# A sparse graph-attention kernel: image tiles, table order, pacing and width of the row gathers in one change

## Chip, cores, metric

The kernel runs on one core of a Trainium2 chip, as one program. The metric is the device time of one execution in microseconds (us).

## What is computed

The input is a feature matrix x (3327 x 128, fp32) and a matrix adj (3327 x 3327) of which about 2% of the entries are not zero. Layer 0 is a four-head attention over the graph, layer 1 a graph convolution; each works on normalised features and adds to x.

```
h = relu(layernorm(x))
for each head:                               # w1, w2, a, Wlin differ by head
    E   = leaky_relu((h @ w1)[:, None] + (h @ w2)[None, :])   # for each pair of nodes
    s   = exp(8 * tanh((E @ a) / 8)) * adj
    out = leaky_relu((s / s.sum(-1)) @ h @ Wlin.T)
x = x + concat(out of the heads) @ w
h = relu(layernorm(x))
A = D^-1/2 (adj + I) D^-1/2
x = x + relu(A @ (h @ W.T + b))
```

## The kernel before

**Tiling.** Nodes are padded to NP = 3328, which makes NB = 26 blocks of 128 destination rows. Only the non-zero entries of adj are worked on. Each block is done in two halves of 64 rows (`hb` 0 and 1). A half has four fetches of eight tiles (`w` 0 to 3, the tile `g`: 128 partitions x 8 x 720 floats) and one fetch of three tiles for overfull rows (`ge`). In a tile of `g`, partition p holds one neighbour of one of 8 destination rows: 8 rows with 16 neighbours each. Tile t of a half therefore belongs to its rows 8t to 8t+7.

**Tables.** What a neighbour contributes lies as one row of 720 floats (2880 bytes) in DRAM, in `tables[0]` for half 0 and `tables[1]` for half 1. Columns 0 to 63 are the adjacency weights towards the 64 destination rows of the present half, 64 to 191 the features, 192 to 195 a term of the score, 196 a one (for the sum), 197 to 207 more ones that nothing uses, 208 (`PROJ`) to 719 the projection by w2 for four heads. The columns from 64 on are written once, in the opening; columns 0 to 63 are written again for each block by `weights(b, hb)` (L554), one DRAM to DRAM transfer of 3328 rows of 256 bytes on the SP queue, which waits until the gathers of the block before have read that table.

**Gathers.** `gather` (L538) puts into a Python queue one `indirect_dma_start` per tile, eight for a `g` and three for a `ge`, in all 26 x 70 = 1820; on POOL they are one instruction each (L548), and in the steady state POOL does nothing else. There are four `g` buffers and one `ge`. `fetch` (L770) starts the next fetch when a buffer is counted free (`allow`, after the last matmul on it, L645 or L663).

**Pacing.** A hand-written loop walks through 26 x 2 x 9 groups and calls `slot()` six times in each, 108 times in a block; this fixes the program order on all engines. In each slot `trickle` (L795) hands out gathers from the queue at `RATE = 0.7` per slot, and `issue` (L788) makes each of them wait on the newest VectorE instruction of the main line:

```
made = make()
if what is not None and state["pace"] is not None:
    tc.add_manual_dep(made.ins, state["pace"], SYNC, reason="pace")
```

`state["pace"]` is the last L585, so a gather is not issued ahead of the VectorE work that stands before it in program order.

**Main line.** `stage_z` (L562) transposes the gathered projections on TensorE (L573) and VectorE takes the maximum with the destination's projection (L585); `stage_r` (L591) reduces it to scores on TensorE (L597); `finish` (L601) does tanh, exp, weights and the aggregation (L605 to L663); `close` ends a block. Between these steps `advance` runs `prep(b, k)` for the next block in 72 steps: transposes of adj (L349), the lists of neighbours (`cand`, `lists`, L399 to L451) and the indices `idx` (L442) and `idxo` (L511) for the gathers.

**Opening.** Before the first gather, the images of the table rows are made in seven groups of four blocks (the last has two): `norm` (L914; the centred features `cen` of the later blocks on POOL, L930), `features(i)` (L949: `img`, L953 and L955), `turn(i)`, `products(i)` (L971: projections, copies to `img`, L987) and `store(i, t)` (L967: image i to table t, L969). The tile `img` has five buffers. `products(i)` stores image i to table 0 and image i-1 to table 1; `weights(0, 0)` and `weights(0, 1)` come before all of them on the SP queue, and the load of the adjacency of block 1, `load(1)` (L336), after all of them. These tiles lie in the pool `pre`, and the four `g` buffers (pool `pg`) take the room that `pre` gives back. In its first fetches the kernel empties the queue without pacing.

**Tail.** After the last block, layer 1 reads strips of the transposed adjacency into the same `g` buffers and multiplies (L870).

Of the kernel before, what the change touches and what calls it, by code (L numbers as in the profile page):

```python
# [15 lines left out]
P = 128  # L16
# [46 lines left out]
OVT = 3  # L63
ROW = 720
FEAT = 64
PROJ = 208
WORK = 133
# [160 lines left out]
def _sparse_layers(tc, nc, x, adj, w1, w2, a, wlin, w, gw, gb, gb_sb, gwT, x_sb, dinv, flag, ident, out):  # L228
# [24 lines left out]
    with ExitStack() as l0:  # L253
# [18 lines left out]
        hoff = res.tile([P, 2], F32, name="hoff")  # L272
        lower = res.tile([P, P], F32, name="lower")
        rowid = res.tile([P, 1], F32, name="rowid")

# [14 lines left out]
        nc.gpsimd.iota(code, [[-1, NP]], base=NP, channel_multiplier=0, allow_small_or_imprecise_dtypes=True)  # L290
        nc.gpsimd.iota(epos, [[-P, 2 * OVT]], base=2 * NP, channel_multiplier=-1, allow_small_or_imprecise_dtypes=True)


# [44 lines left out]
        def prep(b, k):  # L338
# [6 lines left out]
            def tables_step(j0):  # L345
                n = min(4, NB - j0)
                pt = ps_tr.tile([P, 4, P], F32, name="tr")
                for q in range(n):
                    nc.tensor.transpose(pt[:, q, :], adjb[:, (j0 + q) * P:(j0 + q + 1) * P], ident)  # L349
                at = pat.tile([P, 4, P], F32, name="at") if b else blks[0].pool.tile([P, 4, P], F32, name="at0", bufs=4)  # L350
                nc.scalar.copy(at[:, :n, :], pt[:, :n, :])  # L351
                at0 = (b // 4) * NP
                eng = nc.scalar if b else nc.sync
                eng.dma_start(AT_d[at0 + j0 * P:at0 + (j0 + n) * P, b % 4 * P:b % 4 * P + P].rearrange("(b p) c -> p b c", p=P),
                                  at[:, :n, :])
                js = range(min(n, finished(b) - j0))
                if len(js):
                    known.append(known_step(j0, js, at))
# [56 lines left out]
            k.turned = True  # L415
            hTb = pb.tile([P, P], F32, name="hTb")
            nc.sync.dma_start(hTb, hT_d[:, b * P:(b + 1) * P])
            nc.scalar.activation(adjb, adjb, AF.Copy, accum_out=deg)
# [22 lines left out]
            idx = pb.tile([P, NW, 16], mybir.dt.int32, name="idx")  # L441
            nc.vector.tensor_scalar(idx, pm[:, :64].rearrange("p (c t) -> p c t", c=4), -1.0, float(NP), op0=OP.mult, op1=OP.add)  # L442
            k.idx = idx
# [66 lines left out]
            idxo = pb.tile([P, 2, OVT], mybir.dt.int32, name="idxo")  # L510
            nc.vector.tensor_scalar(idxo.rearrange("p c t -> p (c t)"), hits, -1.0, float(NP), op0=OP.mult, op1=OP.add)  # L511
            k.idxo, k.ex = idxo, ex
# [21 lines left out]
            nc.scalar.copy(pex, pm[:, :16 * H].rearrange("p (t h) -> p t h", h=H))  # L534
            k.x1b, k.x1n, k.pex, k.hTb = x1b, x1n, pex, hTb
            yield

        def gather(b, hb, w):  # L538

            k = blks[b]  # L540
            tab = tables[hb]
            if w == NW:
                g, n, at = pe_.tile([P, OVT, ROW], F32, name="ge"), OVT, k.idxo[:, hb]
            else:
                g, n, at = pg.tile([P, WT, ROW], F32, name="g"), WT, k.idx[:, w, WT * hb:WT * hb + WT]

            def one(t):
                return nc.gpsimd.indirect_dma_start(out=g[:, t, :], out_offset=None, in_=tab[:, :],  # L548
                                                    in_offset=bass.IndirectOffsetOnAxis(ap=at[:, t:t + 1], axis=0))

            queue.extend((k, hb, w, partial(one, t)) for t in range(n))
            k.g[hb, w] = g
# [9 lines left out]
        def stage_z(k, hb, m, slot):  # L562
# [4 lines left out]
            for hp in range(2):  # L567
# [13 lines left out]
                if m == 8:  # L581
                    nc.scalar.activation(r[:, :, :n], z[:, :, :n], AF.Relu)  # L582
                else:
                    r0 = HALF * hb + 32 * (m % 2)
                    made = nc.vector.tensor_tensor(r.rearrange("p h (i s) -> p h i s", s=16), z.rearrange("p h (i s) -> p h i s", s=16),  # L585
                                            k.x1n[:, 2 * hp:2 * hp + 2, r0:r0 + 32, None].to_broadcast([P, 2, 32, 16]), OP.max)
                    state["pace"] = made.ins.name
                out.append(r)
# [165 lines left out]
        state = {"slot": 0, "fetched": 0, "g": 4, "ge": 1}  # L754
        state["pace"], state["credit"] = None, 0.0
        RATE = 0.7
        SYNC = mybir.DependencyInfo(mybir.DependencyClass.Sync, mybir.DependencyReason.DATA)
        ends, tails = [], []
# [29 lines left out]
        def issue():  # L788

            what, _, _, make = queue.popleft()  # L790
            made = make()
            if what is not None and state["pace"] is not None:
                tc.add_manual_dep(made.ins, state["pace"], SYNC, reason="pace")

        def trickle():  # L795
            state["credit"] = min(2.0, state["credit"] + RATE) if queue else 0.0
            while queue and (state["credit"] >= 1 or queue[0][0] is None):
                state["credit"] -= queue[0][0] is not None
                issue()
# [20 lines left out]
        def strip(s, j0, n):  # L820
            g = pg.tile([P, WT, ROW], F32, name="g")
            v = g.rearrange("p t c -> p (t c)")[:, :n * 4 * P].rearrange("p (j i) -> p j i", j=n)
# [60 lines left out]

        with tc.tile_pool(name="pre", bufs=1) as pre:
            blks[0].pool = pre
            w2_sb = pre.tile([P, H, D], F32, name="w2_sb")
            nc.scalar.dma_start(w2_sb, w2.rearrange("h k d -> k h d"))
            a_bc = pre.tile([P, H, D], F32, name="a_bc")
            spans = [(lo, min(hi, NB)) for lo, hi in ((0, 4), (4, 12), (12, NB)) if lo < NB]
            x_v = x.rearrange("(b p) d -> p b d", p=P)  # L890
            for lo, hi in spans:
# [16 lines left out]
            wa = pre.tile([P, 3 * H], F32, name="wa")  # L908
            zero = pre.tile([1, ROW // 6], F32, name="zero")
            nc.vector.memset(zero, 0.0)  # L910
            nc.sync.dma_start(tables[0][NP:NP + 1, :].rearrange("r (k u) -> r k u", k=6), zero[:, None, :].to_broadcast([1, 6, ROW // 6]))
            nc.sync.dma_start(tables[1][NP:NP + 1, :].rearrange("r (k u) -> r k u", k=6), zero[:, None, :].to_broadcast([1, 6, ROW // 6]))

            def norm(b0, n):  # L914
# [10 lines left out]
                for _ in inv_root(rstd, var):  # L925
                    pass
                cen = pre.tile([P, n, D], F32, name=f"cen{b0}")
                for k in range(n):
# [6 lines left out]
            def weights_of_scores():  # L935


                prod = pre.tile([P, H, D], F32, name="prod")
                nc.vector.tensor_mul(prod, w2_sb, a_bc)
# [9 lines left out]
            def features(i):  # L949

                b0, n = 4 * i, min(4, NB - 4 * i)
                img = pre.tile([P, 4, ROW - FEAT], F32, name="img", bufs=5)
                nc.gpsimd.memset(img[:, :n, P + H:PROJ - FEAT], 1.0)  # L953
                cen, rstd = normed.pop(b0)
                nc.vector.tensor_mul(img[:, :n, :P], cen, rstd[:, :, None].to_broadcast([P, n, D]))  # L955
                imgs[i] = img

            def turn(i):
                b0, n = 4 * i, min(4, NB - 4 * i)
                pt = ps_s.tile([P, BANK], F32, name="s")  # L960
                for k in range(n):
                    nc.tensor.transpose(pt[:, k * P:(k + 1) * P], imgs[i][:, k, :P], ident)
                hTs[i] = pre.tile([P, BANK], F32, name="hT", bufs=2)
                nc.scalar.copy(hTs[i][:, :n * P], pt[:, :n * P])
# [6 lines left out]
            def products(i):  # L971
# [13 lines left out]
                for k0, pz in zip(range(0, n, 2), pzs):  # L985
                    m = min(2, n - k0)
                    nc.scalar.copy(img[:, k0:k0 + m, PROJ - FEAT:], pz[:, :m, :])  # L987
                nc.scalar.copy(img[:, :n, P:P + H], px[:, :n, :H])
                nc.scalar.copy(p_all[:, b0:b0 + n, :], px[:, :n, H:])
                store(i, 0)  # L990
                if i:
                    store(i - 1, 1)

            wlin_sb = pre.tile([P, H, D], F32, name="wlin_sb")
            nc.sync.dma_start(wlin_sb, wlin.rearrange("h o d -> o h d"))
# [23 lines left out]
            with tc.manual_schedule():  # L1019
# [17 lines left out]
                weights(0, 0)  # L1037
                weights(0, 1)
                turn(0)
                weights_of_scores()  # L1040
                if len(spans):
# [8 lines left out]
                for i in range(1, K):  # L1050
# [3 lines left out]
                    advance(2 + NCODE * i / (K - 1))  # L1054
                    ahead(i + 4)
                store(K - 1, 1)
                advance(NLIST)
                turn_parameters()
                if NB > 1:
                    load(1)  # L1060
                advance(NPREP)

        pg = l0.enter_context(tc.tile_pool(name="pg", bufs=4))

# [165 lines left out]
```

## Time and profile before

| | |
|---|---|
| time, median of 3 runs | 2569.97 us (2569.47 to 2570.88) |
| time of the profiled execution | 3185.3 us, span 3183.6 us |
| busy: PE / DVE / ACT / POOL | 2551.2 / 2055.1 / 691.6 / 1801.2 us |
| granted TensorE clock, mean | 0.912 |
| moved by DMA | 867.74 MB, of it 671.04 MB by the gathers (q0) |
| gathers | 1664 of `g`, 980 ns mean, and 156 of `ge`, 948 ns mean |
| first and last gather | 86.7 us and 3043.4 us |

The profiled execution took 615 us more than the median, so the stages of the profile are longer than those of a plain run by a quarter on average, and waits in it need not be waits of a plain run. "Busy" of POOL is the time in which it makes the descriptors of a gather; when the data have landed is seen from the DMA packets.

### The profile page before, as it was taken

What the parts mean: (1) busy time and instruction counts of PE and PEld (TensorE: products, weight loads), DVE (VectorE), ACT (ScalarE), POOL (GpSimd) and SP (SyncE); (2) the same over time, 40 slices, a digit from 0 to 9 for tenths busy, and PEclk for the clock granted to TensorE, in tenths of its full rate; (3) what the DMA queues carried; (4) which work ended last, traced back from release to release, by engine and by line L of the source; (5) the groups of instructions that cost most, each with busy time, mean ns of one, the idle gap of its engine ahead of it and who ended that gap; (6) DMA issues with size and microseconds to landing.
All of it is one profiled execution on the core that took longest, in us unless ns stands there. A gap on an engine that the chain in (4) does not pass through costs nothing.

```text
span 3183.6 us, 52428 instructions
## 1 busy us (share of the span) xinstructions
PE 2551.2 (80%) x19410; PEld 1758.0 (55%) x19410; DVE 2055.1 (65%) x6256; ACT 691.6 (22%) x1648; POOL 1801.2 (57%) x1865
## 2 busy tenths in 40 slices
PE   5478778878877878887888888788888888888788
PEld 3355555555555655555555565566655556555544
DVE  6466666667676766766667676776666766765432
ACT  3122222122222222222222221222222222221110
POOL 2456565665666666665656566556555655656610
PEclk8688999989999999998999988999899999999899
DMA  9888898888889888888988888888898887988776
GB/s 325 273 272 264 273 290 254 280 286 281 256 284 295 259 285 283 274 269 280 300 248 284 287 258 278 286 272 262 274 282 251 278 286 247 289 255 242 247 257 235
DMA packets 459768, 867.74 MB, mean 273 GB/s; under 512 B 208877, under 2 KB 317937, under 8 KB 456177
## 3 DMA queue, kind: packets, MB, share of 16 engines
q0 software_dynamic: 145600, 671.04, 64.4%
q1 hardware_dynamic: 217360, 136.76, 15.3%
q10 hardware_dynamic: 96544, 56.50, 5.8%
q8 instruction: 156, 2.56, 0.3%
q14 instruction: 108, 0.88, 0.1%
HBM read 795.84 MB, written 112.63 MB: 285 GB/s over the span
## 4 chain that ended last, share of the span: by engine, by line
PE 52%; DVE 16%; another core or an unknown queue 15%; issue 8%; ACT 5%; DMA 2%; POOL 1%; DVEq 0%; ACTq 0%; POOLq 0%; SPq 0%
PE z L573 20%; PE s L597 9%; DVE r L585 8%; PE tr L614 4%; PE z L576 3%; PE z L870 3%; PE ag L645 2%; ACT r L582 2%; DVE cand L399 2%; PE tr L364 1%; PE tr L349 1%; PE ag L663 1%; PE tr L496 1%; ACT ssb L605 1%
## 5 line engine op out<-in xcount | busy, mean ns | idle before, releaser
L548 POOL DMA_INDIRECT g<-table,idx x1664 | 1630.7, 980 | 1113.5 <-issue 429.4
L573 PE MATMUL z<-ident,g 128*128 128x128 f32 x6656 | 1033.0, 301 | 285.6 <-issue 153.0
L585 DVE TENSOR_TENSOR r<-z,x1n 128x1024 f32<-128x1024 f32 x832 | 1013.0, 1219 | 253.4 <-remote 120.8
L573 PEld LDWEIGHTS z<-ident,g 128*128 128x128 f32 x6656 | 845.4, 156 | 499.8 <-issue 249.4
L597 PE MATMUL s<-r,sel 128*32 128x512 f32 (+1 forms) x3744 | 542.0, 617 | 9.3 <-issue 7.0
L617 DVE TENSOR_TENSOR sc<-tr,g 128x32 f32<-128x32 f32 x208 | 39.5, 190 | 645.3 <-PE tr L614 448.9
L614 PE MATMUL tr<-ident,ssb 128*128 128x128 f32 x988 | 181.8, 311 | 164.3 <-ACT ssb L605 110.0
L605 ACT COPY ssb<-s 128x512 f32<-128x512 f32 x260 | 147.0, 565 | 666.0 <-PE s L597 349.5
L614 PEld LDWEIGHTS tr<-ident,ssb 128*128 128x128 f32 x988 | 124.8, 157 | 201.9 <-ACT ssb L605 139.9
L645 PE MATMUL ag<-g,wt 128*32 128x133 f32 x3328 | 179.6, 282 | 66.8 <-issue 66.5
L645 PEld LDWEIGHTS ag<-g,wt 128*32 128x32 f32 x3328 | 113.1, 111 | 209.6 <-issue 199.0
L399 DVE MAX8 cand<-codes 128x8 f32<-128x52 uint16 x1664 | 216.4, 211 | 0.0
L548 POOL DMA_INDIRECT ge<-table,idxo x156 | 147.8, 948 | 94.7 <-DVE r L585 62.3
L351 ACT COPY at<-tr 128x512 f32<-128x512 f32 (+1 forms) x182 | 101.1, 555 | 323.6 <-PE tr L349 111.2
L576 PE MATMUL z<-oi,x1b 128*128 128x384 f32 x416 | 169.3, 488 | 0.8 <-issue 0.7
L597 PEld LDWEIGHTS s<-r,sel 128*32 128x32 f32 x3744 | 81.8, 110 | 150.8 <-issue 130.1
L625 ACT ACTIVATE th<-sc 128x32 f32<-128x32 f32 x260 | 58.3, 224 | 476.3 <-issue 180.1
L582 ACT ACTIVATE r<-z 128x768 f32<-128x768 f32 x104 | 83.8, 813 | 312.1 <-remote 140.7
L349 PE MATMUL tr<-ident,adjb 128*128 128x128 f32 x676 | 112.3, 287 | 22.6 <-DMA adjb<-in_adj_dram 10.6
L573 PEld LDWEIGHTS z<-ident,ge 128*128 128x128 f32 x624 | 78.1, 144 | 81.4 <-issue 38.2
L573 PE MATMUL z<-ident,ge 128*128 128x128 f32 x624 | 105.3, 277 | 5.8 <-DVE r L585 3.9
L364 PE MATMUL tr<-at,x_sb 128*128 128x128 f32 x488 | 75.8, 298 | 35.0 <-ACT at L351 30.1
(177 smaller groups left out, 2426.2 us busy)
## 6 DMA issues: line engine op xcount, KB each, us to landing
adjb<-in_adj_dram SPq DMA_DIRECT2D x26, 1664.0 KB
table<-AT_d SPq DMA_DIRECT2D x52, 832.0 KB
AT_d<-at ACTq DMA_DIRECT2D x150, 256.0 KB
g<-table,idx POOLq DMA_INDIRECT x1664
table<-img SPq DMA_DIRECT2D x12, 1312.0 KB
g<-AT_d SPq DMA_DIRECT2D x11, 1024.0 KB
g<-AT_d ACTq DMA_DIRECT2D x9, 1024.0 KB
g<-AT_d SPq DMA_DIRECT2D x7, 768.0 KB
```

Of the source, the lines that this page charges most:

```text
L349: nc.tensor.transpose(pt[:, q, :], adjb[:, (j0 + q) * P:(j0 + q + 1) * P], ident)
L364: nc.tensor.matmul(pq[:, :P], x_sb[:, j0 + q, :], at[:, q, :], start=(q == 0), stop=(q == js[-1]))
L399: nc.vector.max(cand[:, c, 8:].rearrange("p (r s) -> p r s", s=32)[:, :, sgm % 32], codes.rearrange("p a b -> p (a b)")[:, sgm % 32 * SEG: ...
L548: return nc.gpsimd.indirect_dma_start(out=g[:, t, :], out_offset=None, in_=tab[:, :], in_offset=bass.IndirectOffsetOnAxis(ap=at[:, t:t + 1 ...
L573: nc.tensor.matmul(z[:, i, q * P:(q + 1) * P], g[:, m % 2 * 4 + q, PROJ + h * D:PROJ + (h + 1) * D], ident, is_transpose=True, start=(q == ...
L576: nc.tensor.matmul(z[:, i, :n], k.x1b[:, h * D:(h + 1) * D], k.oi[:, hb * n:(hb + 1) * n], start=False, stop=True, skip_group_check=True)
L582: nc.scalar.activation(r[:, :, :n], z[:, :, :n], AF.Relu)
L585: made = nc.vector.tensor_tensor(r.rearrange("p h (i s) -> p h i s", s=16), z.rearrange("p h (i s) -> p h i s", s=16), k.x1n[:, 2 * hp:2 * ...
L597: nc.tensor.matmul(k.s[32 * h:32 * h + 32, :n], sel[:, h, 31 - at:63 - at], rs[h // 2][:, h % 2, :n], start=(at == 0), stop=(at == 1 or m ...
L605: nc.scalar.copy(ssb[:, :nk * P], s[:, :nk * P])
L614: nc.tensor.transpose(pt[:, q, :], ssb[:, q * P:(q + 1) * P], ident)
L645: nc.tensor.matmul(ag[32 * cg:32 * cg + 32, u, :WORK], wt[:, t].rearrange("p h q -> p (h q)"), g[:, t, FEAT:FEAT + WORK], start=(w == 0 an ...
```

## The change

1. **Images.** Each of the seven images has a pool of its own (`room`), in place of five buffers in turn; `w2_sb`, `a_bc`, `prod`, `wlin_sb`, part of `cen`, `hT` and `at0` borrow room from tiles that the main line uses later. The `g` buffers become four pools of one buffer (`pgs`), taken in turn by `rows_in`; the first lies over the small tiles and image 0, the second over images 1 to 3, the third over 4 and 5, the fourth over 6.
2. **Order on SP.** `products(i)` stores to table 0 alone. After all of these come the seven stores to table 1, with `load(1)` after the second of them, and then `weights(0, 1)`. `hTb` of block 0 is loaded early.
3. **Pacing** is gone: `trickle` empties the queue, and no gather waits on L585.
4. **Columns.** `PROJ` is 197 and a row ends at `COLS = 709`; the stride stays 720. Tile t of a `g` is read from column 16 * (t // 2), so tiles 0 to 7 read 709, 709, 693, 693, 677, 677, 661 and 661 floats, a `ge` 709. The indices count floats in place of rows.

```diff
+COLS = 709
-PROJ = 208
+PROJ = 197
...
+        nc.gpsimd.iota(first, [[0, 2], [16, 4], [0, 2]], ...)
+        nc.vector.tensor_scalar(first, first, float(NP * ROW), None, op0=OP.add)
...
             idx = pb.tile([P, NW, 16], mybir.dt.int32, name="idx")
-            nc.vector.tensor_scalar(idx, pm[:, :64]..., -1.0, float(NP), op0=OP.mult, op1=OP.add)
+            nc.vector.scalar_tensor_tensor(idx, pm[:, :64]..., -float(ROW),
+                                           first[:, None, :].to_broadcast([P, NW, 16]), op0=OP.mult, op1=OP.add)
...
+        def rows_in():
+            state["turn"] += 1
+            return pgs[state["turn"] % 4].tile([P, WT, ROW], F32, name="g")
...
-            tab = tables[hb]
+            tab = tables[hb].rearrange("r (c u) -> (r c) u", u=1)
...
-                g, n, at = pg.tile([P, WT, ROW], F32, name="g"), WT, k.idx[:, w, WT * hb:WT * hb + WT]
+                g, n, at = rows_in(), WT, k.idx[:, w, WT * hb:WT * hb + WT]
             def one(t):
-                return nc.gpsimd.indirect_dma_start(out=g[:, t, :], out_offset=None, in_=tab[:, :],
+                lo = 16 * (t // 2) if w < NW else 0
+                return nc.gpsimd.indirect_dma_start(out=g[:, t, lo:COLS], out_offset=None, in_=tab,
                                                     in_offset=bass.IndirectOffsetOnAxis(ap=at[:, t:t + 1], axis=0))
...
         def issue():
-            what, _, _, make = queue.popleft()
-            made = make()
-            if what is not None and state["pace"] is not None:
-                tc.add_manual_dep(made.ins, state["pace"], SYNC, reason="pace")
+            queue.popleft()[-1]()
         def trickle():
-            state["credit"] = min(2.0, state["credit"] + RATE) if queue else 0.0
-            while queue and (state["credit"] >= 1 or queue[0][0] is None):
-                state["credit"] -= queue[0][0] is not None
+            while queue:
                 issue()
...
+            room = [images.enter_context(tc.tile_pool(name=f"image{i}", bufs=1)).tile(
+                        [P, min(4, NB - 4 * i), ROW - FEAT], F32, name=f"img{i}") for i in range(-(-NB // 4))]
...
             def features(i):
-                img = pre.tile([P, 4, ROW - FEAT], F32, name="img", bufs=5)
+                img = room[i]
                 nc.gpsimd.memset(img[:, :n, P + H:PROJ - FEAT], 1.0)
+                nc.gpsimd.memset(img[:, :, COLS - FEAT:], 0.0)
...
             def products(i):
...
                 store(i, 0)
-                if i:
-                    store(i - 1, 1)
...
                 weights(0, 0)
-                weights(0, 1)
                 turn(0)
+                blks[0].hTb = pb.tile([P, P], F32, name="hTb")
+                nc.sync.dma_start(blks[0].hTb, hT_d[:, :P])
...
-                    ahead(i + 4)
-                store(K - 1, 1)
+                    ahead(i + 3)
+                for i in range(K):
+                    store(i, 1)
+                    if i == min(1, K - 1) and NB > 1:
+                        load(1)
+                weights(0, 1)
                 advance(NLIST)
                 turn_parameters()
-                if NB > 1:
-                    load(1)
                 advance(NPREP)
-        pg = l0.enter_context(tc.tile_pool(name="pg", bufs=4))
+        pgs = [l0.enter_context(tc.tile_pool(name=f"pg{i}", bufs=1)) for i in range(4)]
```

More of the change, by code (lines that the diff above doesn't have):

```diff
@@ L273, in _sparse_layers @@
         lower = res.tile([P, P], F32, name="lower")
+        first = res.tile([P, 16], F32, name="first")
         rowid = res.tile([P, 1], F32, name="rowid")
@@ L291, in _sparse_layers @@
         nc.gpsimd.iota(epos, [[-P, 2 * OVT]], base=2 * NP, channel_multiplier=-1, allow_small_or_imprecise_dtypes=True)
+        nc.gpsimd.iota(first, [[0, 2], [16, 4], [0, 2]], base=0, channel_multiplier=0, allow_small_or_imprecise_dtypes=True)
+        nc.vector.tensor_scalar(first, first, float(NP * ROW), None, op0=OP.add)
         nc.gpsimd.iota(rowid, [[0, 1]], base=0, channel_multiplier=1, allow_small_or_imprecise_dtypes=True)
@@ L349, in tables_step @@
                     nc.tensor.transpose(pt[:, q, :], adjb[:, (j0 + q) * P:(j0 + q + 1) * P], ident)
-                at = pat.tile([P, 4, P], F32, name="at") if b else blks[0].pool.tile([P, 4, P], F32, name="at0", bufs=4)
+                at = pat.tile([P, 4, P], F32, name="at") if b else blks[0].at[j0 // 4 % 4]
                 nc.scalar.copy(at[:, :n, :], pt[:, :n, :])
@@ L415, in prep @@
             k.turned = True
-            hTb = pb.tile([P, P], F32, name="hTb")
-            nc.sync.dma_start(hTb, hT_d[:, b * P:(b + 1) * P])
+            if b:
+                k.hTb = pb.tile([P, P], F32, name="hTb")
+                nc.sync.dma_start(k.hTb, hT_d[:, b * P:(b + 1) * P])
+            hTb = k.hTb
             nc.scalar.activation(adjb, adjb, AF.Copy, accum_out=deg)
@@ L441, in prep @@
             idx = pb.tile([P, NW, 16], mybir.dt.int32, name="idx")
-            nc.vector.tensor_scalar(idx, pm[:, :64].rearrange("p (c t) -> p c t", c=4), -1.0, float(NP), op0=OP.mult, op1=OP.add)
+            nc.vector.scalar_tensor_tensor(idx, pm[:, :64].rearrange("p (c t) -> p c t", c=4), -float(ROW),
+                                           first[:, None, :].to_broadcast([P, NW, 16]), op0=OP.mult, op1=OP.add)
             k.idx = idx
@@ L510, in prep @@
             idxo = pb.tile([P, 2, OVT], mybir.dt.int32, name="idxo")
-            nc.vector.tensor_scalar(idxo.rearrange("p c t -> p (c t)"), hits, -1.0, float(NP), op0=OP.mult, op1=OP.add)
+            nc.vector.tensor_scalar(idxo.rearrange("p c t -> p (c t)"), hits, -float(ROW), float(NP * ROW), op0=OP.mult, op1=OP.add)
             k.idxo, k.ex = idxo, ex
@@ L534, in prep @@
             nc.scalar.copy(pex, pm[:, :16 * H].rearrange("p (t h) -> p t h", h=H))
-            k.x1b, k.x1n, k.pex, k.hTb = x1b, x1n, pex, hTb
+            k.x1b, k.x1n, k.pex = x1b, x1n, pex
             yield
+        def rows_in():
+            state["turn"] += 1
+            return pgs[state["turn"] % 4].tile([P, WT, ROW], F32, name="g")
         def gather(b, hb, w):
             k = blks[b]
-            tab = tables[hb]
+            tab = tables[hb].rearrange("r (c u) -> (r c) u", u=1)
             if w == NW:
@@ L584, in stage_z @@
                     r0 = HALF * hb + 32 * (m % 2)
-                    made = nc.vector.tensor_tensor(r.rearrange("p h (i s) -> p h i s", s=16), z.rearrange("p h (i s) -> p h i s", s=16),
+                    nc.vector.tensor_tensor(r.rearrange("p h (i s) -> p h i s", s=16), z.rearrange("p h (i s) -> p h i s", s=16),
                                             k.x1n[:, 2 * hp:2 * hp + 2, r0:r0 + 32, None].to_broadcast([P, 2, 32, 16]), OP.max)
-                    state["pace"] = made.ins.name
                 out.append(r)
@@ L754, in _sparse_layers @@
         state = {"slot": 0, "fetched": 0, "g": 4, "ge": 1}
-        state["pace"], state["credit"] = None, 0.0
-        RATE = 0.7
-        SYNC = mybir.DependencyInfo(mybir.DependencyClass.Sync, mybir.DependencyReason.DATA)
+        state["turn"] = -1
         ends, tails = [], []
@@ L820, in strip @@
         def strip(s, j0, n):
-            g = pg.tile([P, WT, ROW], F32, name="g")
+            g = rows_in()
             v = g.rearrange("p t c -> p (t c)")[:, :n * 4 * P].rearrange("p (j i) -> p j i", j=n)
@@ L882, in _sparse_layers @@
         fetches = [(b, hb, w) for b in range(NB) for hb in range(2) for w in range(NW + 1)] + [(NB, 0, i) for i in range(len(pieces))]
-        with tc.tile_pool(name="pre", bufs=1) as pre:
-            blks[0].pool = pre
-            w2_sb = pre.tile([P, H, D], F32, name="w2_sb")
+        with tc.tile_pool(name="pre", bufs=1) as pre, ExitStack() as images:
+            lent = pe_.tile([P, OVT, ROW], F32, name="ge").rearrange("p t c -> p (t c)")[:, :16 * P]
+            blks[0].at = list(lent.rearrange("p (i k c) -> p i k c", i=4, k=4)[:, i] for i in range(4))
+            lent = [pr.tile([P, 2, BANK], F32, name=name) for name in ("r0", "r1", "r0", "r1")]
+            w2_sb, a_bc, prod, wlin_sb = (t[:, i].rearrange("p (h d) -> p h d", h=H) for t in lent[2:] for i in range(2))
             nc.scalar.dma_start(w2_sb, w2.rearrange("h k d -> k h d"))
-            a_bc = pre.tile([P, H, D], F32, name="a_bc")
             spans = [(lo, min(hi, NB)) for lo, hi in ((0, 4), (4, 12), (12, NB)) if lo < NB]
             x_v = x.rearrange("(b p) d -> p b d", p=P)
+            cens = {lo: pre.tile([P, hi - lo, D], F32, name=f"cen{lo}") for lo, hi in spans if lo != 4}
+            cens[4] = lent[0].rearrange("p k (b d) -> p (k b) d", d=D)
+            turned = [lent[1][:, i] for i in range(2)]
+            room = [images.enter_context(tc.tile_pool(name=f"image{i}", bufs=1)).tile(
+                        [P, min(4, NB - 4 * i), ROW - FEAT], F32, name=f"img{i}") for i in range(-(-NB // 4))]
             for lo, hi in spans:
@@ L908, in _sparse_layers @@
             wa = pre.tile([P, 3 * H], F32, name="wa")
-            zero = pre.tile([1, ROW // 6], F32, name="zero")
+            zero = pre.tile([1, ROW // 3], F32, name="zero")
             nc.vector.memset(zero, 0.0)
-            nc.sync.dma_start(tables[0][NP:NP + 1, :].rearrange("r (k u) -> r k u", k=6), zero[:, None, :].to_broadcast([1, 6, ROW // 6]))
-            nc.sync.dma_start(tables[1][NP:NP + 1, :].rearrange("r (k u) -> r k u", k=6), zero[:, None, :].to_broadcast([1, 6, ROW // 6]))
+            nc.sync.dma_start(tables[0][NP:NP + 1, :].rearrange("r (k u) -> r k u", k=3), zero[:, None, :].to_broadcast([1, 3, ROW // 3]))
+            nc.sync.dma_start(tables[1][NP:NP + 1, :].rearrange("r (k u) -> r k u", k=3), zero[:, None, :].to_broadcast([1, 3, ROW // 3]))
             def norm(b0, n):
@@ L926, in norm @@
                     pass
-                cen = pre.tile([P, n, D], F32, name=f"cen{b0}")
+                cen = cens[b0]
                 for k in range(n):
@@ L935, in weights_of_scores @@
             def weights_of_scores():
-                prod = pre.tile([P, H, D], F32, name="prod")
                 nc.vector.tensor_mul(prod, w2_sb, a_bc)
@@ L962, in turn @@
                     nc.tensor.transpose(pt[:, k * P:(k + 1) * P], imgs[i][:, k, :P], ident)
-                hTs[i] = pre.tile([P, BANK], F32, name="hT", bufs=2)
+                hTs[i] = turned[i % 2]
                 nc.scalar.copy(hTs[i][:, :n * P], pt[:, :n * P])
@@ L986, in products @@
                     m = min(2, n - k0)
-                    nc.scalar.copy(img[:, k0:k0 + m, PROJ - FEAT:], pz[:, :m, :])
+                    nc.scalar.copy(img[:, k0:k0 + m, PROJ - FEAT:COLS - FEAT], pz[:, :m, :])
                 nc.scalar.copy(img[:, :n, P:P + H], px[:, :n, :H])
@@ L990, in products @@
                 store(i, 0)
-                if i:
-                    store(i - 1, 1)
-            wlin_sb = pre.tile([P, H, D], F32, name="wlin_sb")
             nc.sync.dma_start(wlin_sb, wlin.rearrange("h o d -> o h d"))
```

## The prediction

> **What bounds the kernel now.** I read the page's busy row first, then the chain of waits, then the waits of POOL, and last the timeline of the opening.
>
> ```profile
> PE 2551.2 (80%) x19410; PEld 1758.0 (55%) x19410; DVE 2055.1 (65%) x6256; ACT 691.6 (22%) x1648; POOL 1801.2 (57%) x1865
> ...
> q0 software_dynamic: 145600, 671.04, 64.4%
> ...
> PE 52%; DVE 16%; another core or an unknown queue 15%; issue 8%; ACT 5%; DMA 2%; POOL 1%; DVEq 0%; ACTq 0%; POOLq 0%; SPq 0%
> ```
>
> No engine is full. The chain runs through PE and DVE, the main line of transposes and maxima; POOL and DMA, which all gathers use, hold 3% of it. In the profiled execution the gathers are early: from the packets of q0, the last gather of a fetch has landed 5 to 15 us before the first transpose (L573) that reads it, from block 1 on, and the first gather of a fetch is issued some 22 us before that transpose. But that execution took 3185.3 us (span 3183.6, 1.7 around it) against a median of 2569.97, 19% less. What of the gathers doesn't shrink with the main line may bind in a plain run. So POOL's rate matters:
>
> ```profile
> POOL g L548 <- issue: 429.4, 1180, 20.9
> POOL g L548 <- DVE r L585: 141.1, 119, 3.2
> POOL g L548 <- PE ag L645: 124.5, 59, 3.3
> ```
> ```profile
> 99.06 0.95 POOL L548 DMA_INDIRECT g<-table,idx  x1 [0.30 <-issue]
> 100.31 0.95 POOL L548 DMA_INDIRECT g<-table,idx  x1 [0.30 <-issue]
> ```
>
> Back-to-back gathers stand 1.254 us apart, 0.95 busy and 0.30 of issue. Of 1664 `g` gathers 1180 had only such an issue gap before them; pacing (the wait on L585) held 119 of them and 50 of the `ge`, 203.5 us in all. All 1820 at 1.254 us are 2282 us, 87.8 us of the 113 us that a block takes in the profile. With 86.7 us before the first gather and 140.2 us after the last (3183.6 - 3043.4) this makes 2509 us, a floor for a POOL that never waits: only 61 us under the median. In a plain run the main line and POOL are thus close to each other, and I can't tell from the profile which leads.
>
> The opening is another matter:
>
> ```profile
> 31.94 42.21 SPq L969 DMA_DIRECT2D table<-img  x14
> ...
> 75.98 1.18 SPq L336 DMA_DIRECT2D adjb<-in_adj_dram  x1
> ```
> ```profile
> 50.71 0.69 DVE L955 TENSOR_TENSOR img<-cen,rstd 128x512 f32<-128x512 f32 x1 [8.13 <-DMA table<-img]
> 57.57 0.43 DVE L955 TENSOR_TENSOR img<-cen,rstd 128x256 f32<-128x256 f32 x1 [4.46 <-DMA table<-img]
> ```
> ```profile
> 40.00:80.00 40.00, 24.51 (x94) 14.94 (x92) 23.37 (x126) 14.33 (x26) 3.34 (x8) 0.80 1.04 394
> ```
>
> From 32 us on fourteen image stores fill the DMA engines (share 1.04, 394 GB/s). DVE waits 12.6 us for an `img` buffer. `idx` is ready at 73.8 us, yet the first gather is at 86.7, since it waits until the last store to table 1 has landed at 85.5 us: `g` takes the room of all images.
>
> **What the Trainium skill says.** "DMA: Bandwidth & Descriptors", Why small descriptors are slow and Where 436 GB/s comes from: an engine moves 32-byte beats at 850 MHz, with some 3 cycles more for each descriptor. A gather is 4 packets of two 2880-byte rows and one of 4 bytes on each of 16 engines; (180 + 6) cycles are 219 ns, and the trace has 220 as the median of such packets (279 as the mean, with those that met other traffic). "Perfetto Trace Analysis", DMA Instruction, SWDGE: the end shown of a gather is that of the descriptors. The trace agrees: 0.95 us on POOL, a median of 4.3 us from issue to landing. "SBUF — State Buffer", Operand start alignment: fp32 operands may start at any multiple of 4 bytes; it gives no price. No part of this trace shows the 208-to-197 move of the projections.
>
> **The change part by part.**
>
> *Columns.* A `g` row falls from 720 to 685 floats on average, a `ge` row to 709: 1664 x 128 x 140 bytes and 156 x 128 x 44 bytes, 30.7 of 867.7 MB. By the page's formula, an estimate, a packet falls to 210 ns, so each engine saves 4 x 9.6 ns x 1664 = 64 us and 2 us for `ge`. POOL still makes 128 descriptors a gather, so its 1.254 us stay. At the median packet a gather uses an engine for 0.889 us, 71% of POOL's step: the DMA saving lies beside POOL, unless packets queue behind the weights' transfer (L558, 52 of them), where the gathers wait some 5 us. Taken: 0. Bounds: -20 (a third of the saving reaches the path), and 0 above. The extra operations (`first`, 7 memsets, a two-input `idx`) are at most 0.2 us each, in the opening or beside the gathers. The projections are read by L573's weight loads at an address that is no longer a multiple of 64 bytes: 0 taken; 5 ns on 7280 loads, half of them on the chain, would be +18.
>
> *Images and order.* DVE's waits of 8.1 and 4.5 us go, so `idx` is ready near 61 us and `idxo` near 74. What is late next is DMA. One table is 22.9 us of stores per engine (6656 packets of 2624 bytes at 110 ns for both, over 16). Products are 4.7 us apart, a store 3.5, so table 0 lands near 62 us. By the semaphores of the built kernel the first fetch waits for table 0, `idx` and the table 1 store of image 0, so it starts near 67 us, 20 earlier. But the second fetch waits for the store of image 3, the third for that of 5, the fourth for that of 6, and these come on SP behind `load(1)`, which waits for L418 of block 0 (ACT, about 62 us) and moves 4.4 us of data. With POOL's packets sharing the engines the four fetches start near 67, 89, 104 and 114 us; the last `ge` of half 0 is issued near 128, against 131.7 before. So the 20 us shrink to 4: the same bytes cross a full DMA. Taken -4. Bounds: -20 (all of the lead holds, if stores drain as fast as in the profile's 40 to 80 us), +5 (`load(1)` holds the five stores behind it until 70 us, if L418 stays where it was). Queued behind these on SP are `weights(0, 1)` and block 1's `hTb`; the first is needed by half 1's gathers alone, after 128 us.
>
> *Pacing.* POOL loses the wait on L585; nothing but gathers is queued on POOL. PE, DVE and ACT keep their order in the steady state. A gather can now be early by the time a fetch was stretched: 8 gathers at 0.7 per slot are 11.4 slots of 12. In a plain run a slot is at most 2570 / (26 x 108) = 0.92 us, so 10.5 us against POOL's own 10.0: where slots are short pacing never held POOL, where they are long (list building in `prep`) it did. The lead of a fetch shrinks from 5 to 15 us in the profile by 19% of its 22, to 1 to 11 us, so some fetches are late in a plain run. POOL's idle time between first and last gather, without the 0.30 us of issue, is 2956.7 - 2282 = 675 us; pacing's 203.5 are 30% of it. Taken: 0.3 of the 61 us above the floor, and a little for the ends of fetches that land sooner with shorter rows: -21. Bounds: 0 and -61.
>
> **Sum.** -4 - 21 = -25: 2545 us for the median. In the profiled execution, with its long leads, only the opening and some of the pacing show: about 3185 - 4 - 10 = 3170 there.
>
> **Rivals.**
>
> *A. Opening alone* (2566). The main line leads in a plain run as in the profile, so pacing and columns are hidden and -4 is left. For it: POOL and DMA have 3% of the chain. Against: the floor is 61 us away.
>
> *B. POOL leads throughout* (2505). All idle time of POOL beyond the floor was pacing or its result: 2509 - 4. Against: 59 gathers waited for L645, which frees the buffer, and this stays.
>
> *C. Bursts hold PE* (2607, slower). In the first fetches, which aren't paced before either, PE and DVE stand:
>
> ```profile
> 133.59 1.22 DVE L585 TENSOR_TENSOR r<-z,x1n 128x1024 f32<-128x1024 f32 x1 [23.81 <-remote]
> ```
>
> 26 gathers came at 1.25 us in that time, and PE went on as they ended. If bursts do this to PE in a plain run, then every one of 208 fetches, now issued in one burst of 10 us, may cost something. At 0.3 us each this is +62, with the -25 it makes +37; from 25 / 208 = 0.12 us a fetch it decides. Against: 1180 gathers were in bursts anyhow, and the 615 us between profile and median suggest that standing PE is a matter of profiling. The unaligned loads would add to it.
>
> *D. The change doesn't do what it says:* an index that counts floats could be served float by float. The built kernel has one run of 709 floats per index, so this gets no share of its own.
>
> **How the numbers follow.** Forecast (-10 to -45) 0.42; A 0.21, B 0.17, C 0.20. 0.2% of the time, about what a measurement of this kernel tells from no change, is 5.1 us. A lies across it: half faster, half the same. Faster: 0.42 + 0.17 + 0.10 = 0.69; same 0.11; slower 0.20. The range leaves out half of C and the far end of B: 2505 to 2590. Cases of faster hold most of it; the forecast's own range is 2525 to 2560.
>
> **What would show it right or wrong.** First gather near 67 us with gaps before the 9th and 17th; no DVE wait at L955 for a store; q0 at 640 MB with a median packet near 210 ns; no wait of POOL on L585, and more on L645 and L663 instead; the time from first gather to last shorter by 10 us or more. Wrong: a POOL step other than 1.25 us, transposes L573 with longer loads than 156 ns, longer "remote" waits of PE's readers, or the last gather of half 0 after 132 us.

## The result, and the profile after

The changed kernel takes 2553.82 us (median of 6 runs, 2549.98 to 2559.24) against 2570.38 for the kernel before: a ratio of 0.9938, 95% interval 0.9926 to 0.9951, or 16 us less. A gain of 25 us had been forecast. In three of the four jobs of experiments every kernel, the one before included, took some 600 us more (before 3154, 3155 and 3197 us instead of 2570, as in its first profile, and once on the very chip that gave 2570 in another job), so each experiment is set against the kernel before in its own job, and the two groups of jobs are not mixed.

The page of the profiled execution after (its own time 2552.72, span 2550.9):

```profile
PE 2288.7 (90%) x19410; PEld 1593.6 (62%) x19410; DVE 2027.8 (79%) x6257; ACT 702.8 (28%) x1648; POOL 1793.4 (70%) x1873
...
q0 software_dynamic: 145600, 640.34, 71.0%
...
L561 POOL DMA_INDIRECT g<-table,idx x1664 | 1617.5, 972 | 557.4 <-issue 450.0
...
L586 PEld LDWEIGHTS z<-ident,g 128*128 128x128 f32 x6656 | 745.4, 142 | 368.0 <-DVE r L598 225.7
```

PE looks like the bound with 90%. It isn't; the waits of POOL tell (in us, how often, the longest):

```profile
POOL g L561 <- issue: 450.0, 1460, 2.0
POOL ge L561 <- issue: 35.6, 117, 0.3
POOL g L561 <- DVE miss L490: 24.6, 1, 24.6
POOL g L561 <- DMA table<-img: 12.8, 1, 12.8
...
POOL g L561 <- PE ag L657: 2.7, 2, 2.0
```

After the two long waits, which belong to the opening, POOL waits for almost nothing: L657, which frees a `g` buffer, costs 2.7 us in all. ("issue" is the 0.30 us that stands between any two gathers.) One gather follows the other to the end of the kernel. The other side of it: in five of the ten fetches of a block the last gather lands, in the median, 1.3 to 2.5 us *after* PE has started on the first rows of that fetch, and in 70% of all fetches it is less than 1 us ahead of that transpose. From the 71st gather (171.0 us) to the last (2416.9) the mean step is 1.2841 us: 171.0 + 1749 x 1.2841 + 134.0 (what is left after the last gather starts) = 2550.9, the span. **POOL sets the pace**, and the other kernels with 1820 gathers that take about 2560 us can be read with these three terms too.

The opening, first SP, then POOL, then DVE:

```profile
31.23 29.90 SPq L981 DMA_DIRECT2D table<-img  x9
61.54 1.02 SPq L341 DMA_DIRECT2D adjb<-in_adj_dram  x1
62.60 22.77 SPq L981 DMA_DIRECT2D table<-img  x5
```
```profile
67.54 1.47 POOL L561 DMA_INDIRECT g<-table,idx  x1 [24.63 <-DVE miss L490]
...
76.82 1.14 POOL L561 DMA_INDIRECT g<-table,idx  x1 [0.30 <-issue]
90.77 0.94 POOL L561 DMA_INDIRECT g<-table,idx  x1 [12.81 <-DMA table<-img]
```
```profile
43.76 0.68 DVE L967 TENSOR_TENSOR img<-cen,rstd 128x512 f32<-128x512 f32 x1
47.16 0.41 DVE L967 TENSOR_TENSOR img<-cen,rstd 128x256 f32<-128x256 f32 x1
```

DVE no longer waits at the features' product (8.13 and 4.46 us before). The first gather starts 19 us sooner than in the profile of before, and the ninth then stands 12.81 us for a store of table 1, behind `load(1)` on SP.

### The profile page after: what moved, and what is told of

Read it like the earlier page. It is cut to its first block, busy times and chain, and to the rows that moved or that the text cites. A ratio compares the mean times of both kernels' runs of the same rounds, so it can differ in the third digit from the quotient of the medians.

```text
span 2550.9 us, 51928 instructions
## 1 busy us (share of the span) xinstructions
PE 2288.7 (90%) x19410; PEld 1593.6 (62%) x19410; DVE 2027.8 (79%) x6257; ACT 702.8 (28%) x1648; POOL 1793.4 (70%) x1873
## 2 busy tenths in 40 slices
DMA packets 459750, 837.00 MB, mean 328 GB/s; under 512 B 208858, under 2 KB 317924, under 8 KB 456164
## 5 line engine op out<-in xcount | busy, mean ns | idle before, releaser
L586 PE MATMUL z<-ident,g 128*128 128x128 f32 x6656 | 926.8, 279 | 162.2 <-DVE r L598 109.6
L598 DVE TENSOR_TENSOR r<-z,x1n 128x1024 f32<-128x1024 f32 x832 | 1009.4, 1215 | 46.3 <-PE z L586 44.4
L586 PEld LDWEIGHTS z<-ident,g 128*128 128x128 f32 x6656 | 745.4, 142 | 368.0 <-DVE r L598 225.7
L609 PE MATMUL s<-r,sel 128*32 128x512 f32 (+1 forms) x3744 | 491.1, 597 | 0.7 <-ACT ssb L617 0.7
L657 PEld LDWEIGHTS ag<-g,wt 128*32 128x32 f32 x3328 | 99.2, 111 | 115.3 <-issue 100.5
L626 PE MATMUL tr<-ident,ssb 128*128 128x128 f32 x988 | 154.5, 277 | 3.9 <-ACT ssb L617 3.5
L586 PEld LDWEIGHTS z<-ident,ge 128*128 128x128 f32 x624 | 81.5, 146 | 99.8 <-issue 28.6
L609 PEld LDWEIGHTS s<-r,sel 128*32 128x32 f32 x3744 | 73.8, 108 | 110.4 <-issue 86.3
L586 PE MATMUL z<-ident,ge 128*128 128x128 f32 x624 | 112.7, 284 | 24.3 <-DMA ge<-table,idxo 21.3
L657 PE MATMUL ag<-g,wt 128*32 128x133 f32 x3328 | 133.7, 279 | 0.0
L626 PEld LDWEIGHTS tr<-ident,ssb 128*128 128x128 f32 x988 | 115.2, 142 | 15.2 <-ACT ssb L617 14.4
L400 DVE SCALAR_TENSOR_TENSOR codes<-adjb,code 128x832 uint16<-128x832 f32 x104 | 102.2, 1020 | 1.8 <-DMA adjb<-in_adj_dram 1.8
```

The source lines that it names most:

```text
L400: nc.vector.scalar_tensor_tensor(codes[:, i], adjb[:, c0:c0 + part], 0.0, code[:, c0:c0 + part], op0=OP.not_equal, op1=OP.mult, accum_out= ...
L586: nc.tensor.matmul(z[:, i, q * P:(q + 1) * P], g[:, m % 2 * 4 + q, PROJ + h * D:PROJ + (h + 1) * D], ident, is_transpose=True, start=(q == ...
L609: nc.tensor.matmul(k.s[32 * h:32 * h + 32, :n], sel[:, h, 31 - at:63 - at], rs[h // 2][:, h % 2, :n], start=(at == 0), stop=(at == 1 or m ...
L626: nc.tensor.transpose(pt[:, q, :], ssb[:, q * P:(q + 1) * P], ident)
L657: nc.tensor.matmul(ag[32 * cg:32 * cg + 32, u, :WORK], wt[:, t].rearrange("p h q -> p (h q)"), g[:, t, FEAT:FEAT + WORK], start=(w == 0 an ...
```

## The experiments

**A second profile of before.** No edit.

> The kernel before, unchanged, once more, for a second profile of it (the first took 615 us longer than the median). Theory P (POOL's gathers set the pace of a plain run, before and after): the profiled time is near 2570, gathers stand at a mean of about 1.30 us from the 36th to the last, a sum that is POOL's own 1.28 (0.977 busy, 0.305 issue) and some tens of us of waits, part of them on L585. Rival M (PE and DVE set the pace): fetches land 2 us or more ahead of their first transpose in most blocks and POOL waits over 100 us for L645 and L585. Rival H (the bytes set the pace): DMA share 0.98 or more in the steady state, and issue to landing well over the 4.3 us median of the first profile.

Measured: 3161.9 us (28 runs of before in this job: median 3153.7). Step from the 71st gather on 1.606 us, of which 0.973 busy; fetches land 6 to 14 us early; DMA share 0.88 between 500 and 2000 us:

```profile
POOL g L548 <- issue: 410.3, 1153, 19.2
POOL g L548 <- DVE r L585: 145.5, 130, 2.9
POOL g L548 <- PE ag L645: 120.9, 60, 3.5
```

This is rival M's picture: at this time the main line leads and POOL follows it. The first profile was thus no accident of one execution; it shows the kernel as it runs in such a job, not as it runs at 2570. One difference can be seen: ACT's copy of the scores (`ssb`) starts a median of 0.62 us after PE's last matmul for it, and in 66 of 260 cases over 1 us after both that matmul and ACT's own last instruction; in the profile after it is 0.07 us and one case. (An expectation further on has 87 cases; the trace does not give that number again.) PE's results are seen late, and the profile names no one for it. PE's mean clock is 0.91 instead of 0.98, and semaphore records are missing (2137 for 2380 matmuls that set one, against 2402 for 2409 after). What makes a whole job run at this time stays open.

**Pacing removed, alone** (in the kernel before):

```diff
-            what, _, _, make = queue.popleft()
-            made = make()
-            if what is not None and state["pace"] is not None:
-                tc.add_manual_dep(made.ins, state["pace"], SYNC, reason="pace")
+            queue.popleft()[-1]()
...
-            state["credit"] = min(2.0, state["credit"] + RATE) if queue else 0.0
-            while queue and (state["credit"] >= 1 or queue[0][0] is None):
-                state["credit"] -= queue[0][0] is not None
+            while queue:
```

> The kernel before without the pacing alone. P: the waits on L585 go and nothing replaces them: 0.2 to 0.5% faster (2557 to 2565). M: no difference within 0.1%. H: no difference within 0.1%. Bursts that hold PE: slower, by 0.3% or more.

Measured: 3264.5 against 3153.7, ratio 1.0348 (1.0322 to 1.0375): 110 us slower. All theories but the bursts miss the sign here. POOL's waits on L585 are gone, and a larger one has come:

```profile
POOL g L548 <- PE ag L644: 561.9, 175, 18.9
POOL g L548 <- issue: 429.8, 1385, 4.4
POOL ge L548 <- PE ag L662: 73.9, 10, 8.3
```

A block takes 116.5 us instead of 112.5 (blocks 1 to 24). Divided into its 18 groups, most groups that got more gathers got longer (the second: 3.2 to 5.0 gathers, 5.0 to 8.0 us), and two that lost 1.5 got shorter (the seventeenth: 5.7 to 4.2 gathers, 8.9 to 6.4 us). Over 16 groups the change in gathers and the change in time have a correlation of 0.86. The two groups left out, in which fewer than one gather is left, speak against it: they lost 3.2 and 2.8 gathers and got no more than 0.2 us shorter, and over all 18 groups the correlation is 0.60. A longer group also has room for more gathers. It is rival C's picture, bursts during which PE doesn't get on; that the bursts cause it is not shown.

**Shorter rows, alone** (in the kernel before: COLS = 709, PROJ = 197, indices that count floats, lo as in the change).

> The kernel before with the shorter rows alone (25 to 35 floats fewer a row, projections at column 197); pacing and opening as before. P and M: within 0.15% of before, for POOL makes as many descriptors. H: 30.7 of 868 MB go, 64 us of each DMA engine: 0.6 to 2.5% faster (2506 to 2555), that is, all of the change's 16 us or more.

Measured: 3155.1, ratio 0.9999 (0.9987 to 1.0010). As P and M had it, and not as H did. At a DMA share of 0.87, 30.7 MB less are worth nothing, and the projections' new place costs nothing either: L579's weight loads take 154 ns against 155 before.

**The opening, alone** (the changed kernel with pacing and whole rows put back).

> The changed kernel with the pacing put back and whole rows of 720 floats fetched: the new opening is left (and the projections at column 197). P: what the 36th gather gains, 126 against 132 us in the profiles: 0.2 to 0.3% faster (2562 to 2565). M: all of the change, 0.6% (2554). H: 0.2%, as P. If the second fetch's wait for the stores costs what the first one's lead brings: no difference.

Measured: 3139.0, ratio 0.9951 (0.9927 to 0.9976), 15 us: between what P and H (0.2 to 0.3%) and M (0.6%) had, and the interval reaches both. The 71st gather starts at 199.0 us against 209.3 in the profile of before from the same job: 10 of the 15.

**The changed kernel, once more.**

> The changed kernel, unchanged, once more. In the runs just made the kernel before took 3153.7 us where it had taken 2570; so this is to tell whether the comparison holds there too. Theory S (there are two regimes, and the change's parts add up in each): where before takes about 3150, the sum of the parts just measured, unpaced +3.5%, opening -0.5%, columns 0: about 3.0% slower, 3247 us; where before takes 2570: 0.6% faster. Rival T (the regime goes with the kernel, not with the place): 2554 whatever before takes. Rival U (short rows or the new opening undo what the missing pacing costs): within 0.5% of 3153.

Measured: 3253.2 against 3155.3, ratio 1.0306 (1.0288 to 1.0324). Theory S, 3247, holds; T and U fall. The same change is 0.6% faster in one job and 3.1% slower in another. Where it is slower, POOL has the wait that the missing pacing alone brought (561.9 us there):

```profile
POOL g L561 <- PE ag L657: 578.3, 170, 14.3
POOL g L561 <- issue: 431.1, 1388, 4.8
```

The next four ran together, with before at 2569.7 us; they are the ones that explain the result.

**Pacing put back** (into the changed kernel).

> The changed kernel with the pacing put back (opening and short rows stay). Theory S, parts add up: where before takes about 3150, 0.5% faster than before, as the opening alone was; that is 3.5% faster than the whole change. Where before takes 2570 (theory P, POOL sets the pace): slower than the changed kernel's 2554 by 5 to 10 us, 0.2 to 0.4% faster than before. Rival (pacing costs only with the old opening or with whole rows): no different from the changed kernel.

Measured: 2560.2, ratio 0.9962 (0.9948 to 0.9977). Against the change's 0.9938 the pacing costs 0.24%, 6 us. The trace has the same amount: a step of 1.2877 instead of 1.2841, over 1749 steps 6.3 us. Its waits are short, since L598 is nearly always done when a late POOL gets there; from the 71st gather on, the gaps between gathers grow by 2.9 us. The larger part, 3.5 us, lies in longer gathers, those of `ge` above all (first the changed kernel, then this one):

```profile
L561 POOL DMA_INDIRECT ge<-table,idxo x156 | 152.6, 978 | 47.5 <-issue 35.6
```
```profile
L561 POOL DMA_INDIRECT ge<-table,idxo x156 | 156.6, 1004 | 47.5 <-issue 32.0
...
POOL g L561 <- issue: 363.0, 1182, 2.1
POOL g L561 <- DMA g<-table,idx: 37.7, 120, 1.5
...
POOL g L561 <- DVE r L598: 21.5, 67, 1.4
```

The intervals of the two ratios leave some 5 us on either side of the 6.

**Whole rows** (in the changed kernel, 720 floats from column 0; PROJ stays at 197):

```diff
-        nc.gpsimd.iota(first, [[0, 2], [16, 4], [0, 2]], base=0, channel_multiplier=0, allow_small_or_imprecise_dtypes=True)
+        nc.gpsimd.iota(first, [[0, 2], [0, 4], [0, 2]], base=0, channel_multiplier=0, allow_small_or_imprecise_dtypes=True)
...
-                lo = 16 * (t // 2) if w < NW else 0
-                return nc.gpsimd.indirect_dma_start(out=g[:, t, lo:COLS], out_offset=None, in_=tab,
+                return nc.gpsimd.indirect_dma_start(out=g[:, t, :], out_offset=None, in_=tab,
```

> The changed kernel fetching whole rows of 720 floats (30.7 MB more). P and S: as the changed kernel, within 0.2% (3.1% slower than a before of 3150, 0.6% faster than one of 2570). Rival H (bytes): slower than the changed kernel by 0.6% or more. Rival J (shorter bursts soften what the missing pacing costs): slower than the changed kernel by 0.3% or more where before takes 3150 only.

Measured: 2562.4, ratio 0.9972 (0.9958 to 0.9985): 0.34% or 9 us slower than the change, more than P and S allowed, less than H asked. The trace has 6 of it: the 71st gather at 173.1 us instead of 171.0, a step of 1.2864 instead of 1.2841 (4.0 us over 1749). The DMA engines are full here:

```profile
500.00:2000.00 1500.00, 1370.92 (x12258) 973.62 (x12251) 1272.38 (x3934) 437.96 (x1030) 1136.52 (x1169) 0.99 0.99 335
```
```profile
500.00:2000.00 1500.00, 1374.13 (x12253) 976.29 (x12254) 1267.48 (x3923) 438.75 (x1032) 1136.18 (x1168) 0.99 1.00 348
```

(First the changed kernel, then the one with whole rows; the columns are busy us of PE, PEld, DVE, ACT and POOL with their instructions, then PE's clock, DMA share and GB/s.) With whole rows the gathers land later, a median of 5.19 us after their issue instead of 4.99, and from the 71st on the gaps between them are 4.9 us longer in all, while the gathers themselves are 1.0 us shorter. That the gaps grow because of the landings fits this, and is not shown apart.

**Fewer gathers on POOL** (in the changed kernel):

```diff
-            queue.extend((k, hb, w, partial(one, t)) for t in range(n))
+            if w == NW:
+                queue.append((k, hb, w, partial(nc.sync.dma_start, g[:, :, :COLS], tables[hb][:OVT * P, :].rearrange("(t p) c -> p t c", p=P)[:, :, :COLS])))
+            else:
+                queue.extend((k, hb, w, partial(one, t)) for t in range(n))
```

This kernel reads the table's first 384 rows for every `ge`, in place of the listed ones, so what it computes is other.

> The changed kernel with the rows of each ge tile fetched by one plain DMA on SP from the table's first 384 rows in place of three gathers on POOL from the listed rows (so the rows past the first lists are others); bytes are the same, POOL issues 1664 gathers in place of 1820, about 200 us less work. P, where before takes 2570: 3 to 8% faster than the changed kernel, until PE or DMA is next. Where before takes 3150 the gathers land 8 us or more early, so POOL isn't the bound: within 1% of the changed kernel there. Rival H: within 0.5% of the changed kernel in either place.

Measured: 2516.6, ratio 0.9784 (0.9769 to 0.9800), 37 us faster than the change (40 by the ratios). That POOL was the bound is shown: as many bytes are moved (837.00 MB), the DMA share is 1.00, the gathers that are left land no sooner (a median of 5.38 us after their issue, 4.99 in the changed kernel), and what went are 156 of POOL's instructions. But of 200 us of POOL's work only 37 come out, about half of the least that P expected, for the next bound is close behind:

```profile
POOL g L561 <- issue: 419.8, 1374, 0.8
POOL g L561 <- PE ag L660: 168.6, 86, 7.1
```

POOL now waits 168.6 us for PE to free buffers: the main line leads. A block takes 88.6 us, and 90.0 in the changed kernel, where POOL's gathers set it.

**The weights' transfers left out** (of the kernel before; all adjacency weights are written as ones, once, so what it computes is other).

> The kernel before with the edge weights of both tables set to one once, and the 52 transfers of 3328 pieces of 256 bytes from AT_d left out. Theory W (where before takes 3150, PE's results are seen late mainly while these small packets cross the DMA engines): under 2950 us, and waits of ACT for the scores over 1 us beyond PE's end drop from 87 of 260 to under 30. Rival N (lateness is everywhere): within 3% of before, over 60 such waits stay.

Measured: 2564.3, ratio 0.9977 (0.9966 to 0.9988). The two theories spoke of a job at 3150, and this ran at 2570, so neither is decided; here 52 transfers of 3328 pieces each are worth 5 us. The trace serves in another way: it is the only one with the old opening, pacing and whole rows at this time. 71st gather 175.3, step 1.2889, rest 135.8, span 2565.3.

**The last three** were meant to run at 2570, and ran in a job with before at 3196.5.

> The kernel before, unchanged, for a profile at its time of 2570. Theory P (POOL sets the pace before as after): from the 71st gather to the last a mean step of 1.288 to 1.292 us, as the paced kernel had (1.2877), so 5 to 8 us more than the changed kernel over 1749 steps; the rest of the 16 us lies before the 71st gather (at 175 to 178 us, against 171.0); fetches land within 1 us of their first transpose or after it in most cases. The weight loads of L573 take 142 ns as in the changed kernel, if column 197 costs nothing. Rival M (PE and DVE set the pace): a step of 1.30 or more with over 50 us of waits for L585 or L645.

Measured: 3186.7, step 1.6195, 71st gather at 212.0: the picture of the first two profiles of before. So there is no trace of the kernel before at 2570.

> The new opening alone (pacing and whole rows put back), now at a before of 2570. If the parts add up as in the last runs (opening with short rows 0.38% faster, opening with no pacing 0.28%, all three 0.62%): 0.04% faster, 2569, no difference that can be told. By the prediction: 4 us, 0.16% faster. Rival (the opening is most of it, and the other two overlap): 0.25% or more faster.

Measured: ratio 0.9964 (0.9948 to 0.9979), 12 us, with the 71st gather at 200.5 us, 11.5 before that of before: the opening gain seen above, again. It says nothing of 2570.

> The kernel before with short rows and without pacing, with the old opening. If the parts add up: all but the opening's 1 us, 0.55% faster (2555). By the opening's rival: 0.3% faster or less. Where before takes 3150: 3.5% slower, as the missing pacing alone.

Measured: 3346.1, ratio 1.0467 (1.0440 to 1.0494). More than the 3.5% of the missing pacing alone, although the rows alone did nothing and the whole change lost 3.1%. The parts don't add up here; why stays open.

## Why the prediction was right, and where not

**The sum** was 25 us and is 16: the right sign, and between the forecast's -10 and -45. That is luck in part. The two terms that the prediction counted on, opening and pacing, are worth some 8 us together, less than the forecast's least; the other 9 come from the columns, which it had at 0. No part was measured alone at 2570; what follows comes from taking parts back out of the changed kernel.

**Opening: -4, measured about -2, which can't be told from 0.** First gather near 67: 67.5. A gap before the ninth gather: 12.81 us, for a store behind `load(1)`, as worked out; the one before the seventeenth did not come, since the ninth was late enough for both. The last `ge` of half 0 near 128: 124.1 (130.4 in the profile of before, not 131.7). The 71st gather is at 171.0 against 175.3 in the kernel without weights' transfers, 4.3 us, 2.1 of them owed to the shorter rows (173.1 with whole ones), so about 2 are left for the opening. By ratios, opening and rows have 0.38%, opening and no pacing 0.28%, all three 0.62%, which leaves 0.04%, 1 us, for the opening if the parts add up. Each ratio has an interval of 0.13% or so on either side; the three together leave some 6 us, so the ratios do not tell the opening's gain from none.

**Pacing: -21, measured -6.** The step that failed is the floor. I priced a gather at 1.254 us, read off two lines of a timeline, and so found 61 us between POOL's floor and the median; 0.3 of that, a guess, made most of the 21. The groups of the same page had the mean: 980 ns for a `g` and 948 for a `ge` gather, 1778.5 us of work, and with 0.304 of issue for each of 1820, 553 us, a floor of 1778.5 + 553 + 86.7 + 140.2 = 2558 us. That is 12 us under the median, not 61: POOL had in all likelihood led already before (no trace shows before at 2570; the kernel without weights' transfers, its nearest, has a step of 1.2889), and little was left for pacing to cost. The same error puts rival B at 2505, though its mechanism, POOL leading throughout, is what the profile after shows.

**Columns: 0, measured -9.** I took the saved bytes to lie beside POOL, because the packets of a gather, at their median, fill 71% of POOL's step. I counted only q0. With the other queues the DMA engines are at 0.99 in a run at 2570, and with more bytes the gathers land later (5.19 us instead of 4.99). The bound of -20 held it. The 0 was read off a profile whose DMA share was 0.87, where the rows are worth nothing (0.9999). The median packet of q0 is 214 ns (210 expected, from 220), POOL's bare step is still 1.25 us, so rows addressed by floats are not served float by float (rival D). The unaligned column costs nothing: 142 ns for L586, 143 ns with the old place in the kernel without weights' transfers.

**Rival C, the bursts,** had its price from 0.3 us a fetch, +37 in all. In a job at 2570 it doesn't show: the median `ssb` is 0.07 us behind PE in all four kernels. In a job at 3150 the time fits it, and is larger: +98 us for the change. I set it aside in part because standing PE might be a matter of profiling; but every run there takes as long as the profile. The waits on L657 that were to take the place of those on L598 came only there (578.3 us; 2.7 in the profile after). "Profile near 3170" fails for the same reason: the profile after came from an execution at 2552.72, and in a job at 3155 it is 3254.

**The way to the forecast** from a profile 24% longer than the median went through a guess of what shrinks. The leads of the fetches show how far that missed: 1 to 11 us ahead of the transposes were expected, and in the profile after the median of a fetch lies between 5.0 us ahead and 2.5 us behind. Main line and POOL "close to each other, and I can't tell which leads" was the honest reading, and the kernel with fewer gathers shows how close: 1.4 us in a block of 90.

## What to carry to other kernels

Take the price of a repeated instruction from the mean of its group, not from a clean stretch of a timeline: over 1820 gathers 0.03 us were 50 us, and made a gain of 6 look like one of 21. When a profile takes much longer than the median, find a profile at the median's time before sizing a wait in it; here taking the pacing out was worth -0.24% at one time and +3.5% at the other. And where two resources are both near full, what is taken from the leading one buys only the distance to the next: 200 us off POOL bought 37 us.

## What was not expected of the hardware

**Long gathers.** 150 of 1820 gathers in the profile after take over 1.05 us instead of 0.947, 46 us in all, most of the difference between the bare step (0.947 + 0.304) and the mean. 118 of them (39 us) overlap one of three DVE operations that read two operands from SBUF: `codes` (L400), `oi` (L496) and `wt` (L648); of the 346 gathers that overlap one of these a third are long, of the other 1474 2%. For `codes` and `wt` the order decides: of the 50 gathers that start while `codes` runs 47 are long, of the 46 during which `codes` starts none is; for `wt` it is 59 of 123 and 3 of 115. And one that is long ends a fixed time after the DVE operation, wherever it started: 0.82 us after the end of `codes` (0.815 to 0.821 for the middle 80%), and 0.82 us after `wt` too. The traces with pacing, with whole rows and without the weights' transfers show the same 0.82 us. L598, which reads one of its two operands from PSUM, does not do this: of 787 gathers that start while it runs, 16 are long. From the timeline (other engines' lines left out):

```profile
1003.48 0.42 DVE L648 TENSOR_TENSOR wt<-pe,wq 128x256 f32<-128x256 f32 x1
1003.55 1.16 POOL L561 DMA_INDIRECT g<-table,idx  x1 [0.30 <-issue]
...
1005.02 0.95 POOL L561 DMA_INDIRECT g<-table,idx  x1 [0.30 <-PE z L586]
```

The gather that starts under `wt` takes 1.16 us and ends 0.81 us after it; the next takes 0.95. The Trainium skill, "SBUF — State Buffer", Who interferes with whom, says that a DVE instruction with two SBUF inputs contends with a GpSimd instruction that reads SBUF; the indices of a gather lie there. The trace agrees: a gather that starts second ends as if it had waited for the end of the DVE operation. That it is the reading of the indices that waits is argued, and no run here moved these operations. It would be the next thing to try. The 39 us at stake are about the 37 that fewer gathers bought, after which the main line leads.
